# Five of the first seventeen edge groups get keys and values from gathered node rows instead of gathered table rows

## The chip, the cores and the metric

The kernel runs on one NeuronCore of a Trainium2 chip. The metric is device time in microseconds (us) of one execution. The engines are named as in the profile: PE (matrix products), DVE (vector), ACT (scalar), POOL and SP (here issuers of DMAs, POOL of the indirect ones). The time before is the median of ten runs.

## The reference, cut to what matters

A graph of 3125 nodes with 128 features has 100000 edges, sorted by destination; each edge has one of five relations. There are eight heads of 16 features.

```
for r in range(5):
    q = x[dst] @ W_Q[r];  k = x[src] @ W_K[r];  v = x[src] @ W_V[r]     # per edge
    logits = (q * k).sum(-1) / 4 + attn_bias[r]                         # per edge and head
    attn = softmax of logits over the edges of type r with the same dst
    out += segment_sum(attn * v, dst)                                    # per node
h = out @ out_proj_w.T + out_proj_b + x
x = layernorm(x + layernorm(h) * gamma + beta)
```

## The kernel before, in words

**Build.** For each of 25 blocks of 128 nodes, `turn` transposes the block (L301, L303) and `table` (L312) multiplies it by keys' and values' weights of all five relations; the rows of 256 numbers go to a table in HBM, `kv_d`, one row for each node and relation (store at L319, issued by SP). Between the blocks, the list `side` puts preparation: `rows_of` (L327 to L337) finds for each node which stretch of 500 destinations (SR) holds its first edge, `in_row` (L341) reads that stretch by an indirect DMA of POOL, `count` (L349, ACT) counts in it; the others make the indices `idx`, the places `nkey` and the types, and check the input. The small parameters are loaded after the build (L489 to L494).

**First queries.** For blocks 0 to 2 the nodes are loaded again, turned, multiplied by the query weights (L546, L556), split into three bf16 parts (L561 to L575), and stored to `q_d` (L579), one block after the other.

**Groups.** The edges are handled in 196 groups of 512 (g, 4 tiles of 128 edges). `gather(g)` (L527 to L533) issues four indirect DMAs on POOL, each bringing 128 rows of `kv_d` into one of KVB = 24 buffers. `fetch` (L584 to L590) loads keys and a window of 128 query rows; `spot` (L594) makes one-hot matrices; `spread_q` (L603, twelve bf16 products) brings queries to edges; `logits` (L616, L617) multiplies and reduces; `store_logits` (L622) writes them to `lg_d`. For each block b of nodes, `maxima_load` (L629), an indirect DMA on POOL too, loads the logits of each node's edges as the tile `ell`, and `maxima` (L636 to L673), in two halves, takes the maxima by relation. The weighing of group v then takes `spread_m` (L693), `less_max`, `exps`, `weigh` (L710), `places` (one-hot matrices on ACT, L728 and L731, or on DVE, L723) and `sums` (L744), with the running sum of the group before carried in by a fifth product (L748) from a fifth one-hot plane of `at`. `norm`, `by_node`, `project`, `residual`, `roots` and `norms` finish the nodes.

**Order.** All is unrolled and ordered by hand in steps k; each engine and each DMA queue works in the order in which the loop from L911 issues. Group g has its logits in step `step_of[g]`, which is g, plus one extra step after each group in CATCH_UP = (186, 188, 190, 192, 194). Gathers are issued AHEAD = 3 steps before use, one step before use in the last 16. The load of block b stands on POOL's queue in step `full_step[b] + 1`: the first behind the gathers of group 12, the second behind those of group 21. They need the logits up to group 8 and group 17. The first weighing is in step 16, and steps run to 223; the last group has its logits in step 200 and its weighing in step 214. The gather of group g + 24 must wait until group g has been weighed.

Of the kernel before, what the change touches and what calls it, by code (L numbers as in the profile page):

```python
# [8 lines left out]
F32 = mybir.dt.float32  # L9
# [38 lines left out]
CATCH_UP = (186, 188, 190, 192, 194)  # L48
# [7 lines left out]
SR = 500  # L56
NSR = E // SR
KVB = 24
# [58 lines left out]
def windowed_path(  # L117
# [13 lines left out]
    key_d = dram.tile([NGR, GE], BF16, name="key_d")  # L131

# [5 lines left out]
    nkey = keep("nkey", [P, T + 1, NGR])  # L138
# [11 lines left out]
    wq = keep("wq", [P, R, H])  # L150

# [15 lines left out]
    nc.vector.memset(xn[:, NT - 1, :], 0.0)  # L167
    fr = load.tile([1, NGR + NSR], I32, name="fr")
# [16 lines left out]
    nc.sync.dma_start(xn[:, :4, :], x[: 4 * P].rearrange("(i p) h -> p i h", p=P))  # L185
# [7 lines left out]
    def load_rows(name, a, pad):  # L193
        t = load.tile([HG, 2, GE], I32, name=name)
        nc.vector.memset(t[:, 1, :], pad)
        nc.scalar.dma_start(t[:, 0, :], a[: HG * GE].rearrange("(g i) -> g i", i=GE))
        nc.scalar.dma_start(
            t[: HR - 1, 1, :], a[HG * GE : (NGR - 1) * GE].rearrange("(g i) -> g i", i=GE)
        )
        rest = E - (NGR - 1) * GE  # L200
        nc.gpsimd.dma_start(
            t[HR - 1 : HR, 1, :rest], a[(NGR - 1) * GE :].rearrange("(g i) -> g i", g=1)
        )
        return t
# [30 lines left out]
    mid = iota("mid", [[P * E // N, NT]], NT)  # L235
    five = iota("five", [[R, WN]], WN, mult=-1)
# [21 lines left out]


    wkv = load.tile([P, R, 2, H], F32, name="wkv")  # L260
# [14 lines left out]
    firsts = load.tile([P, NGR + NSR], F32, name="firsts")  # L275
    frf = load.tile([1, NGR + NSR], F32, name="frf")

    def begins():
        nc.vector.tensor_copy(frf, fr)
        fp = pps.tile([P, NGR + NSR], F32, name="fp", tag="tr", bufs=2)  # L280
        nc.tensor.matmul(fp, ones[0:1, :], frf, start=True, stop=True)
        nc.vector.tensor_copy(firsts, fp)
        nc.vector.tensor_copy(first, frf[:, :NGR])
        nc.vector.tensor_scalar_mul(first5, frf[:, :NGR], float(R))
        nc.vector.tensor_tensor(
            nkey[:, T, 1:], firsts[:, 1:NGR], firsts[:, : NGR - 1], op=ALU.subtract
        )
        nc.vector.tensor_scalar(
            nkey[:, T, 1:], nkey[:, T, 1:], float(R), row_of, op0=ALU.mult, op1=ALU.subtract
        )  # L290
# [7 lines left out]

    def turn(b):
        tp = pps.tile([P, P], F32, name="tp", tag="tr", bufs=2)  # L300
        nc.tensor.transpose(tp, xn[:, b, :], ident)  # L301
        xT = work.tile([P, P], F32, name="xT", bufs=4)
        nc.vector.tensor_copy(xT, tp)  # L303
        return xT
# [21 lines left out]
    def rows_of(c0, c1):  # L326
        less = work.tile([P, 5, NSR], BF16, name="less", bufs=1)  # L327
        nc.vector.tensor_tensor(
            less,
            firsts[:, None, NGR:].to_broadcast([P, 5, NSR]),  # L330
            node[:, c0:c1, None].to_broadcast([P, 5, NSR]),
            op=ALU.is_lt,
        )
        g = grp[:, c0:c1]
        nc.vector.tensor_reduce(g, less, AX.X, ALU.add)
        nc.vector.tensor_scalar(g, g, 1.0, 0.0, op0=ALU.subtract, op1=ALU.max)
        nc.vector.tensor_copy(grp_i[:, c0:c1], g)  # L337
# [57 lines left out]
    def put_key(ep, g):  # L395
        nc.scalar.mul(nkey[:, :T, g], ep, -1.0)
# [38 lines left out]
    def checks():  # L435
# [16 lines left out]

    side = {
        0: [begins],
        1: [lambda: rows_of(0, 5)],
        2: [lambda: rows_of(5, 10), lambda: rows_of(10, 15)],
        3: [lambda: rows_of(15, 20)],
        4: [lambda: rows_of(20, NT)],
        5: [keys_a],
        6: [keys_c],  # L460
        7: [lambda: along(kvrow, 0, put_idx)],
        8: [lambda: along(kvrow, 1, put_idx)],
        9: [keys_b],
        11: [lambda: along(keyr, 0, put_key)],
        12: [lambda: along(keyr, 1, put_key)],
        13: [lambda: along(typr, 0, put_typ)],
        14: [lambda: along(typr, 1, put_typ)],
        16: [sorted_rows],
        18: [sorted_ends],
        21: [starts],  # L470
        23: [checks],
    }
    rows, counted = {}, 0
    xT = {b: turn(b) for b in range(2)}
    for b in range(NT):
        if b + 2 < NT:
            xT[b + 2] = turn(b + 2)
        table(b, xT.pop(b))
        for f in side.get(b, ()):
            f()  # L480
        while len(rows) < min(NT, 5 * b) and len(rows) - counted < 8:
            rows[len(rows)] = in_row(len(rows))
        for n in range(2):
            if b >= 3 and counted < len(rows):
                count(counted, rows[counted])
                counted += 1


    nc.scalar.dma_start(beta_t, beta.partition_broadcast(P))  # L489
    nc.scalar.dma_start(gamma_t, gamma.partition_broadcast(P))  # L490
    ow = load.tile([P, H], F32, name="ow")
    nc.scalar.dma_start(ow, out_w)
    nc.scalar.dma_start(bias4, attn_bias.partition_broadcast(P))
    nc.scalar.dma_start(lift, out_b.rearrange("(o h) -> o h", o=1))  # L494
    nc.vector.tensor_scalar_mul(bias4, bias4, 4.0)
    nc.vector.tensor_tensor(lift, lift, beta_t[0:1, :], op=ALU.subtract)
    op_ = pps.tile([P, P], F32, name="op_", tag="tr", bufs=2)
    nc.tensor.transpose(op_, ow, ident)
    nc.scalar.copy(out_wT, op_)
# [27 lines left out]
    def gather(g):  # L527
        kv = kvs_[g % KVB]
        for t in range(T):
            nc.gpsimd.indirect_dma_start(  # L530
                out=kv[:, t, :], out_offset=None, in_=kv_d[:, :],
                in_offset=bass.IndirectOffsetOnAxis(ap=idx[:, t, g : g + 1], axis=0),
            )  # L533


    def fetch_x(name, b):
        n = min(P, N - b * P)
        xb = flow.tile([P, H], F32, name=name, bufs=2 if name == "xq" else 4)
        if n < P:
            nc.vector.memset(xb, 0.0)  # L540
        nc.sync.dma_start(xb[:n], x[b * P : b * P + n, :])
        live[name, b] = xb
# [41 lines left out]
    def fetch(g):  # L584
        kt = flow.tile([P, T, P], BF16, name="kt", bufs=3)
        nc.sync.dma_start(kt.rearrange("w t p -> w (t p)"), key_d[g].partition_broadcast(P))
        qw = flow.tile([P, 3, H], BF16, name="qw", bufs=3)
        f = window(g, first5, SPE)
        nc.sync.dma_start(qw.rearrange("w s h -> w (s h)"), q_d[bass.ds(f, P), :])
        live["kt", g], live["qw", g] = kt, qw  # L590
# [22 lines left out]
    def logits(g):  # L613
        kv, lg = kvs_[g % KVB], live["lg", g]
        prod = flow.tile([P, T, H], F32, name="prod")
# [11 lines left out]
    def maxima_load(b):  # L627
        ell = late_flow.tile([P, D, LW], F32, name="ell")
# [7 lines left out]
    def maxima(b, c0, c1):  # L636
# [17 lines left out]
        wl = late_flow.tile([P, RH, HEADS, D], F32, name="wl", bufs=1)  # L654
# [33 lines left out]
    def spread_m(g):  # L688
        me = ps.tile([P, T, HEADS], F32, name="me")
# [27 lines left out]
    def places(g, on_dve):  # L717

        at = late_flow.tile([P, T + 1, WR], F32, name="at", bufs=3)
        n = T if g == 0 else T + 1  # L720
        for t in range(n):
# [9 lines left out]
        nc.scalar.activation(  # L731
            at[:, on_dve:n, :], at[:, on_dve:n, :], AF.Relu, bias=1.0, scale=-1.0
        )
        live["at", g] = at

    def sums(g, done):
# [3 lines left out]
        if g is not None:  # L740
            at, wv = live.pop(("at", g)), live.pop(("wv", g))
            pp = both[:WR, :PW]
            for t in range(T):
                nc.tensor.matmul(  # L744
                    pp, at[:, t, :], wv[:, t, :], start=(t == 0), stop=(t == T - 1 and g == 0)
                )
            if g:
                nc.tensor.matmul(  # L748
                    pp, at[:WR, T, :], live.pop(("pt", g - 1)), start=False, stop=True
                )  # L750
            live["pp", g] = pp
# [46 lines left out]
    def residual(b):  # L798
# [6 lines left out]
        h = late_flow.tile([P, H], F32, name="h", bufs=4)  # L805
# [49 lines left out]
    def lag(b):  # L855

        return LAG if b < NT - 3 else LAG - 2
# [21 lines left out]

    q_from = []  # L880
# [9 lines left out]
    first_b = [b for b in range(NT) if q_from[b] < 2]  # L890
    for b in first_b:
        fetch_x("xq", b)
        turn_q(b)
        turned(b)
        for c0, c1 in ((0, RH), (RH, R)):
            queries(b, c0, c1)
            first_part()
            remainder()
            second_part()
            third_part()  # L900
        store_q(b)
    nc.scalar.dma_start(
        m_d.rearrange("(p a) c -> p (a c)", p=P), oT.bitcast(BF16)[:, : NT * R * 3 * HEADS]
    )
    for g in range(3):
        fetch(g)
# [4 lines left out]
    for k in range(root_at[NT] + 2):  # L911
        v, g = v_at.get(k), group_at.get(k)
        q_step = {k - f: b for b, f in enumerate(q_from) if b not in first_b and -2 <= k - f <= 5}

        if k + 3 in group_at:
            fetch(group_at[k + 3])
# [11 lines left out]
        for u in range(NGR):  # L928
            if max(at_k[u] - 3, ready[block_of(u)] - 2) == k:
                fetch_m(u)  # L930

# [6 lines left out]

        for b in range(NT):
# [34 lines left out]
        if v_at.get(k + 1) is not None:  # L974
            places(v_at[k + 1], 3 if k >= final - 1 else 0)
# [11 lines left out]
        for b in range(NT + 1):  # L987
            if root_at[b] == k:
                roots(b)
                norms(b)  # L990
        if 0 in q_step:
# [510 lines left out]
```

## Time and profile before

| what | us |
|---|---|
| median of 10 runs (1213.93 to 1219.82) | 1215.58 |
| the profiled execution, its own time | 1217.49 |
| its span in the trace | 1215.7 |
| last table store issued by SP (L319) | 96.5 |
| first gather on POOL (L530) | 101.30 |
| first logits (L616), group 0 | 142.43 |
| logits of group 17 (L616) | 195.67 |
| second load of `ell` on POOL (L629) | 213.42 |
| last gather on POOL | 1131.51 |
| last weighing (L710), group 195 | 1194.91 |

The span falls into the build (0 to 101 us), the groups ahead of the first weighing (to about 190 us), the long middle in which each block of eight groups takes 41.5 us, and the end, which is free of gathers. POOL is busy for 806.0 us, DVE for 937.2, ACT for 728.9, and PE for 806.3. Busy shares are means over these stages.

### The profile page before, as it was taken

To read this page: it belongs to the slowest core of one execution; us is meant where nothing else is said; L and a number is where in the kernel's file an instruction comes from. 1 tells how busy PE (TensorE), PEld (TensorE's weight loads), DVE (VectorE), ACT (ScalarE), POOL (GpSimd) and SP (SyncE) were. 2 spreads that over 40 slices of the span, in tenths; PEclk is the share of its full clock that TensorE was granted. 3 is DMA by queue.
4 is the path that set the end of the run, shared out by engine and by line. 5 is a ranking of instruction groups with operands and counts; after the bars stand their busy time and mean duration, and the time that the engine had idled before them with its cause. 6 is when DMAs were issued, how large, how long until landed. Compare 5 with 4: busy or idle time off the path is not lost.

```text
span 1215.7 us, 25279 instructions
## 1 busy us (share of the span) xinstructions
PE 806.3 (66%) x7503; PEld 698.3 (57%) x7503; DVE 937.2 (77%) x2521; ACT 728.9 (60%) x2441; POOL 806.0 (66%) x902
## 2 busy tenths in 40 slices
PE   5793356558566766767576767566765777668674
PEld 2351236457466655666576657566665667657664
DVE  4742376777888888879888888888888888877775
ACT  1561015357666766766677667666766776669443
POOL 2715777777777777777777777777777777774200
PEclk9896566777678787877887687878877877768666
DMA  7984777667667766776676677677676767655200
GB/s 168 325 328 147 212 215 184 148 181 191 158 171 183 181 170 171 184 178 168 175 191 167 170 180 192 156 172 184 173 178 163 191 172 174 172 138 127 51 9 14
DMA packets 181075, 207.02 MB, mean 170 GB/s; under 512 B 82614, under 2 KB 145871, under 8 KB 180808
## 3 DMA queue, kind: packets, MB, share of 16 engines
q0 software_dynamic: 41392, 116.59, 35.4%
q1 hardware_dynamic: 135112, 84.01, 27.8%
q10 hardware_dynamic: 4424, 4.71, 1.6%
q8 instruction: 62, 1.02, 0.3%
q14 instruction: 85, 0.70, 0.2%
HBM read 169.90 MB, written 35.29 MB: 169 GB/s over the span
## 4 chain that ended last, share of the span: by engine, by line
DVE 28%; DMA 26%; POOL 14%; issue 12%; PE 11%; ACT 8%; SPq 1%; ACTq 0%; DVEq 0%; POOLq 0%
POOL kv L530 13%; DMA kv<-kv_d,idx 11%; DMA ell<-lg_d,start_i 7%; DVE wl L656 4%; DVE lg L617 4%; DVE prod L616 3%; PE pp L744 3%; DVE wv L710 3%; ACT at L728 3%; PE pr L312 2%; DVE mx L662 2%; DVE hot L594 2%; DMA kt<-key_d 1%; PE qe L603 1%; DVE o L769 1%
## 5 line engine op out<-in xcount | busy, mean ns | idle before, releaser
L530 POOL DMA_INDIRECT kv<-kv_d,idx x784 | 747.2, 953 | 274.4 <-issue 194.3
L744 PE MATMUL pp<-wv,at 128*125 128x136 f32 x1568 | 304.2, 351 | 16.5 <-DVE o L769 14.8
L728 ACT ACTIVATE at<-row_at,nkey 128x125 f32<-128x125 f32 x934 | 292.0, 390 | 0.0
L744 PEld LDWEIGHTS pp<-wv,at 128*125 128x125 f32 x1568 | 257.8, 239 | 24.8 <-DVE o L769 17.1
L603 PE MATMUL qe<-qw,hot 125*128 125x128 bf16 x2352 | 211.8, 255 | 30.7 <-DMA qw<-q_d 17.1
L603 PEld LDWEIGHTS <-hot 125*128 125x128 bf16 x2352 | 198.7, 125 | 35.7 <-issue 12.2
L693 PE MATMUL me<-mw,hot 125*128 125x8 bf16 x2352 | 91.3, 168 | 185.1 <-DVE wv L710 124.3
L693 PEld LDWEIGHTS <-hot 125*128 125x128 bf16 x2352 | 83.2, 101 | 223.5 <-DVE wv L710 134.9
L704 ACT ACTIVATE me<-me 128x32 f32<-128x32 f32 x196 | 36.2, 185 | 218.2 <-DVE me L700 217.4
L616 DVE TENSOR_TENSOR prod<-kv,qe 128x512 f32<-128x512 f32 x196 | 134.4, 686 | 36.0 <-PE qe L603 21.8
L710 DVE TENSOR_TENSOR wv<-kv,me 128x512 f32<-128x512 f32 x196 | 133.2, 680 | 20.1 <-ACT wv L705 20.0
L731 ACT ACTIVATE at<-at 128x625 f32<-128x625 f32 (+2 forms) x196 | 137.5, 702 | 6.2
L617 DVE TENSOR_REDUCE lg<-prod 128x32 f32<-128x512 f32 x196 | 134.5, 686 | 6.8
L748 PE MATMUL pp<-pt,at 125*125 125x136 f32 x390 | 101.7, 351 | 29.8 <-ACT pt L760 27.6
L556 PE MATMUL prq<-wq,xTq 128*128 128x384 f32 (+1 forms) x100 | 57.0, 665 | 85.3 <-DVE rem L566 84.1
L748 PEld LDWEIGHTS pp<-pt,at 125*125 125x125 f32 x390 | 79.4, 247 | 35.4 <-ACT pt L760 32.7
L594 DVE TENSOR_SCALAR hot<-kt,row_of 125x512 bf16<-125x512 bf16 x196 | 72.3, 369 | 16.3 <-DMA kt<-key_d 16.3
L754 PEld LDWEIGHTS pp<-rsum,o 125*128 125x128 f32 x392 | 80.1, 248 | 2.2 <-ACT oT L779 1.4
L656 DVE TENSOR_TENSOR wl<-by_head,shut 128x1536 f32<-128x1536 f32 (+1 forms) x50 | 74.6, 1491 | 7.6 <-ACT by_head L641 5.8
L556 PEld LDWEIGHTS prq<-wq,xTq 128*128 128x128 f32 x100 | 21.7, 271 | 94.9 <-DVE rem L566 92.8
L662 DVE TENSOR_REDUCE mx<-wl 128x24 f32<-128x1536 f32 (+1 forms) x50 | 74.3, 1487 | 1.7
L754 PE MATMUL pp<-rsum,o 125*128 125x25 f32 x392 | 71.8, 266 | 2.0 <-DVE o L769 1.3
(158 smaller groups left out, 1006.3 us busy)
## 6 DMA issues: line engine op xcount, KB each, us to landing
kt<-key_d SPq DMA_DIRECT2D x196, 128.0 KB
qw<-q_d SPq DMA_DIRECT2D x196, 96.0 KB
kv_d<-kvs SPq DMA_DIRECT2D x24, 640.0 KB
kv<-kv_d,idx POOLq DMA_INDIRECT x784
q_d<-q SPq DMA_DIRECT2D x25, 480.0 KB
lg_d<-lg SPq DMA_DIRECT2D x196, 18.0 KB
mw<-m_d SPq DMA_DIRECT2D x196, 6.0 KB
xq<-in_x SPq DMA_DIRECT2D x24, 64.0 KB
```

The source lines that it names most:

```text
L530: nc.gpsimd.indirect_dma_start(out=kv[:, t, :], out_offset=None, in_=kv_d[:, :], in_offset=bass.IndirectOffsetOnAxis(ap=idx[:, t, g : g + ...
L603: nc.tensor.matmul(qe[:, t, :], hot[:, t, :], qw[:WR, s, :], start=(s == 0), stop=(s == 2))
L616: nc.vector.tensor_tensor(prod, kv[:, :, :H], live.pop(("qe", g)), op=ALU.mult)
L617: nc.vector.tensor_reduce(lg[:, :, :HEADS], prod.rearrange("p t (k d) -> p t k d", d=HD), AX.X, ALU.add)
L656: nc.vector.tensor_tensor(wl[:, :n], by_head[:, None].to_broadcast([P, n, HEADS, D]), shut[:, :n, None, :].to_broadcast([P, n, HEADS, D]), ...
L693: nc.tensor.matmul(me[:, t, :], hot[:, t, :], mw[:WR, s, :], start=(s == 0), stop=(s == 2))
L710: nc.vector.tensor_tensor(wv[:, :, :H].rearrange("p t (k d) -> p t k d", d=HD), kv[:, :, H:].rearrange("p t (k d) -> p t k d", d=HD), live ...
L728: nc.scalar.activation(at[:, t, :], row_at[:, :WR], AF.Abs, bias=nkey[:, t, g : g + 1], scale=1.0)
L731: nc.scalar.activation(at[:, on_dve:n, :], at[:, on_dve:n, :], AF.Relu, bias=1.0, scale=-1.0)
L744: nc.tensor.matmul(pp, at[:, t, :], wv[:, t, :], start=(t == 0), stop=(t == T - 1 and g == 0))
L748: nc.tensor.matmul(pp, at[:WR, T, :], live.pop(("pt", g - 1)), start=False, stop=True)
L754: nc.tensor.matmul(op, live.pop(("o5", done)), rsum[:WR], start=True, stop=True)
```

## The change: what it does

**Early groups.** XG is the groups 4, 7, 10, 13 and 16. `gather` does nothing for them. Ahead of the row reads of the build, POOL issues 20 indirect DMAs that gather the source nodes' rows of x themselves (512 bytes a row) by `xi`, a list loaded straight from `src`. After the last table store, SP stores them to `x_d` (five stores of 256 KB). For group u, two steps before step u - 4 (for group 4 ahead of the steps), SP loads `xe` from there, and the edge types `tr` as a row given to all partitions. In step u - 4, `turn_x` transposes four tiles on PE, and `by_relation` makes five masked copies on DVE, `xm`. In step u - 3, `products` issues 20 f32 products of 256 columns, which add up over the five relations. In step u - 2, `put_kv` copies keys and values into the buffer of the group on ACT. The tile `xm` has the buffer of the tile `wl` of `maxima` (one buffer, tag "wl"); `tx` and `pk` have the two PSUM buffers of `me`.

**First queries.** The turned blocks 0 to 2 of the build are kept, multiplied by the query weights at once after the last table, in six products that follow each other, and stored.

**Carry.** The fifth plane of `at` goes; a table `carried`, made once in the build, holds for each group a plane of five columns, and the product of the carry is issued ahead of the last of the four products of `sums`.

**Build.** SR is 250; `rows_of` looks at three stretches around the expected one for all blocks at once; the small loads move into the build; the first blocks of x come ahead of the other loads, and a small copy on ACT ahead of the weights.

**Steps.** CATCH_UP is empty, so the last group has its logits in step 195; the last three blocks have a lag of seven steps instead of six. The last weighing is still in step 214, and steps still run to 223. Four blocks instead of three have their roots put off until after the last weighing. `places` puts two planes on DVE instead of three in the end. `xr` and `h` have three buffers, `prod` and `ell` one.

```diff
-CATCH_UP = (186, 188, 190, 192, 194)
+CATCH_UP = ()
-SR = 500
+SR = 250
+SB = P * E // N // SR
+SPAD = 5
+XG = range(4, 17, 3)
+QB = 3
...
+    def rows_of():
+        less = load.tile([P, NT, 3, SB], F32, name="less")
+        rows = firsts.rearrange("p (b s) -> p b s", s=SB)
+        for i in range(3):
+            nc.vector.tensor_tensor(
+                less[:, :, i, :], rows[:, i : i + NT, :],
+                node[:, :, None].to_broadcast([P, NT, SB]), op=ALU.is_lt,
+            )
+        nc.vector.tensor_reduce(grp, less.rearrange("p b i s -> p b (i s)"), AX.X, ALU.add)
...
+    def early_x():
+        i, t = pieces.pop(0)
...
+        nc.gpsimd.indirect_dma_start(
+            out=staged[i][:, t, :], out_offset=None, in_=x[:, :],
+            in_offset=bass.IndirectOffsetOnAxis(ap=xi[:, i, t : t + 1], axis=0),
+        )
...
+    for n in range(20):
+        early_x()
     rows, counted = {}, 0
...
+    put_x(NT)
...
+    for i in pieces:
+        b, c0, c1 = i
+        pr = pps.tile([P, 4, H], F32, name="pr", tag="pr", bufs=4)
+        prs[i] = pr[:, : c1 - c0, :]
+        nc.tensor.matmul(prs[i], kept[b], wq[:, c0:c1, :], start=True, stop=True)
+        nc.scalar.copy(q3s[b][:, c0:c1, 0, :], prs[i])
...
     def gather(g):
+        if g in XG:
+            return
...
+    def by_relation(g):
+        tr, tx = live.pop(("tr", g)), live.pop(("tx", g))
+        xm = late_flow.tile([P, R, T, P], F32, name="xm", tag="wl", bufs=1)
+        for r in range(R):
+            nc.vector.scalar_tensor_tensor(
+                xm[:, r], tr.rearrange("h (p t) -> h t p", t=T), float(r), tx,
+                op0=ALU.is_equal, op1=ALU.mult,
+            )
+    def products(g, t0):
+        xm = live["xm", g]
+        pk = ps.tile([P, 2, KVW], F32, name="pk", tag="me")
+        for t in range(2):
+            for r in range(R):
+                nc.tensor.matmul(
+                    pk[:, t, :], xm[:, r, t0 + t, :], wkv[:, r].rearrange("h s c -> h (s c)"),
+                    start=(r == 0), stop=(r == R - 1),
+                )
+    def put_kv(g, t0):
+        nc.scalar.copy(kvs_[g % KVB][:, t0 : t0 + 2, :], live.pop(("pk", g, t0)))
...
-        n = T if g == 0 else T + 1
-        for t in range(n):
+        for t in range(T):
...
+                if t == T - 2 and g:
+                    nc.tensor.matmul(
+                        pp[:R], carried[:WR, g, :], live.pop(("pt", g - 1)),
+                        start=False, stop=False,
+                    )
...
-        return LAG if b < NT - 3 else LAG - 2
+        return LAG if b < NT - 3 else LAG - 1
...
+    x_at = {g: step_of[g] - 4 for g in XG}
...
-            places(v_at[k + 1], 3 if k >= final - 1 else 0)
+            places(v_at[k + 1], 2 if k >= final - 1 else 0)
```

## Prediction

> **What bounds the kernel now.** First the busy shares by engine: DVE 77%, POOL 66%, nothing near full, so the share alone names no limit. Second the waits of POOL over the whole span:
>
> ```profile
> POOL kv L530 <- issue: 194.3, 637, 0.3
> ...
> POOL ell L629 <- DMA mw<-m_d: 16.7, 1, 16.7
> POOL ell L629 <- ACT lg L610: 13.5, 1, 13.5
> POOL kv L530 <- DMA kv<-kv_d,idx: 9.1, 30, 0.3
> ```
>
> The columns are us in total, times, longest. 637 of the 784 gathers "wait" 0.3 us for nothing that the profile shows: that is the pace of POOL itself. Third its timeline, around the second load of `ell`:
>
> ```profile
> 212.17 0.94 POOL L530 DMA_INDIRECT kv<-kv_d,idx  x1 [0.30 <-issue]
> 213.42 0.95 POOL L629 DMA_INDIRECT ell<-lg_d,start_i  x1 [0.30 <-issue]
> 214.67 0.95 POOL L530 DMA_INDIRECT kv<-kv_d,idx  x1 [0.31 <-issue]
> ```
>
> One indirect DMA takes 0.95 us and the next follows 0.30 later. From the first gather (101.30) to this load stand 89 of them, 112.1 us, so 1.26 us each. The two long waits of the first view stand at 1121 and 1149, in the end. From 101 to 1107 POOL is a chain without a hole (one of 1.9 us): **POOL's count of indirect DMAs is the bound**. Fourth the windows, to see who has room:
>
> ```profile
> 120.00:150.00 30.00, 8.83 (x60) 6.22 (x61) 8.77 (x17) 2.82 (x12) 22.79 (x24) 0.56 0.71 207
> ...
> 180.00:200.00 20.00, 12.57 (x116) 10.65 (x116) 12.90 (x31) 11.09 (x38) 15.12 (x17) 0.50 0.66 176
> ...
> 600.00:800.00 200.00, 138.63 (x1448) 127.07 (x1448) 169.73 (x463) 140.31 (x472) 151.55 (x159) 0.77 0.71 176
> ```
>
> Behind each stretch: its length, busy us of PE, PE's weight loads, DVE, ACT, POOL, then PE's granted clock, DMA share, GB/s. In the middle DVE is at 85%. Fifth DVE's waits between 400 and 1000:
>
> ```profile
> DVE sd L817 <- ACT sd L812: 22.5, 15, 1.6
> DVE mine L643 <- DMA ell<-lg_d,start_i: 20.0, 12, 2.9
> ```
>
> DVE waits about 1.7 us a block for an `ell` that POOL issued in its turn, and never there for a gather to land. So the weighing side is only some 4% (1.7 of 41.5) faster than POOL: a second limit close behind.
>
> **The sum** is made on the span, 1215.7 us; this execution's own time is 1217.49, the median 1215.58, so that a saving on the span is taken off the median unchanged.
>
> *A. Build: -6 (0 to -9).* The old `rows_of` costs DVE five times 1.19 + 1.20 (L328, L335) and small ones, 13 us, while tables wait. The new one is three comparisons of 400 and a sum over 1200 elements: by 0.69 for 512 (L616) and 1.22 for 1024 (L369) about 3, and `carried` 1.2. But POOL, free at 8.1 and used at 30.2 before, first issues 20 gathers of x: 8.2 + 20 x 1.26 = 33.4. That covers them all but 3 us; then come 25 row reads to 65, the last landing near 67.5. Two are counted per table, which holds table 15 there. Nine tables at the cadence of L312 (74.81 to 77.07: 2.26) end at 88; I add 2.5 for stores in the way (one took 7.3 at 62.9): 90.5 for the last store, against 96.5. Bounds: no gain if table stores bind (640 KB per table; 340 GB/s between 60 and 90), -9 without that 2.5 and another 0.5.
>
> *B. Twenty gathers less: -25.2*, 20 x 1.26, all ahead of the second `ell`. Without further waits this load would go at 213.4 - 25.2 - 6 = 182.2.
>
> *C. New waits of POOL at `ell`: +13 (0 to +56).* That load needs the logits of group 17. First queries: before, three blocks in series, the last stored at 131.14, first logits 11.3 later, at 142.4. Now nothing is fetched; from the last table ACT has 3 x (0.48 + 0.37 + 0.51 + 0.40) = 5.3, with first product and DVE some 8, then 11.3 again, and 2 for 1.3 MB of `x_d` stores: first logits at 90.5 + 8 + 11.3 + 2 = 111.8.
> Then each early group is a chain over three steps: `spread_q` 0.84 (L603 x12), logits 1.45, `spot` 0.35, first mask 0.7, then the other masks beside the first tile's products 3.2, then 15 products. The masks are priced at 0.69 (L616, f32 from PSUM; L379 with int32 inputs gives half of 1.22). A product of 256 columns of f32: L312 does 1280 columns in 2.15, so 0.43; 15 make 6.5. Together 13.0. With three chains, 2 for block 3's queries and 1.8 for the first logits, the fourth masking (group 13) begins at 111.8 + 1.8 + 39 + 2 = 154.6. Now `maxima` of block 0 falls in: its `wl` shares a buffer with `xm` and waits for the products (10.4), then 1.76 + 1.75, logits and `spot` 1.8, second half 4.3 (0.6, 1.23, 1.22, six of 0.2): 20, to 174.6. Group 16's masks and products 10.4, `spread_q` 0.84, three logits with what lies between 7: logits of 17 end at 192.8; from logits to `ell` the end of this trace shows 2.4 (1146.8 to 1149.2). The load goes at 195.2 instead of 182.2. It waits 13, partly already at the first load (after logits 8); 18.2 of the saving are left. Behind it POOL is the chain of before, from group 22 on. The lower end is no wait. The upper one is PE at half its pace throughout: 0.43 more on each of 100 products, 43 on top.
>
> *The clock row.* After a gap the six instructions of L312 take 4.17 us, six us later 2.31:
>
> ```profile
> 18.74 4.17 PE L312 MATMUL pr<-wkv,xT 128*128 128x512 f32 x6 [2.49 <-ACT wkv L272]
> ...
> 24.56 2.31 PE L312 MATMUL pr<-wkv,xT 128*128 128x512 f32 x6
> ```
>
> In my chain PE stands still some 1 us between masks, so I take the warm value. [...]
>
> *D. The end: -1 (-7 to +9).* Before, 28 steps from the logits of 186 (1082.2) to the last weighing (1194.9) hold both long waits of POOL. After: nine steps with groups at POOL's pace, 9 x 5.04 + two `ell` 2.5 = 47.9, from 1077.6 (the maxima of block 22, 4.6 here, come a step later); then 19 steps of 2.79 (weighings 185 to 195: 1166.99 to 1194.91), 53, and maxima 13.2: 1191.7, 3.2 less. One more root behind the last weighing costs 2.5 (1201.72 to 1204.2); `xr` with three buffers must wait for one of these roots, about 1; the smaller `places` gives back a little. Bounds: 7 less if these steps keep 2.55 as the fastest do, 9 more if the 3 us load of `xr` (1203.71 in the chain) and two more waits for `ell` stand bare.
>
> *At nothing:* the fifth plane saves ACT 0.39 + about 0.15 in each of 196 steps, where ACT is at 70% in the middle and off the bound; if POOL did not cover it, it would be worth the 0.6 that DVE waits at L710 per block. The carry product comes 0.29 earlier in its accumulation and may wait for the copy `pt` by as much (L748 waits 22.6 in 800 us); DVE covers it. `put_kv`, two ACT copies of 0.59, ends a step before use.
>
> Sum: -6 - 25.2 + 13 - 1 = -19.2: **1196 us**.
>
> **Rivals.**
> *1. POOL never waits at `ell`.* For it: PE's bare work per three steps is 8.6 + 2.5 + 0.7 = 11.8, gathers take 10.1, and queries may start sooner than 111.8. Against: one buffer for `xm` and `wl`. C falls away: 1183.
> *2. The weighing side binds.* The chain takes 15.5 instead of 13 (cold starts, strided masks), 12.5 more over five, or, being only 4% faster than POOL, it does not catch up the 9 us that it is later against POOL than in the middle (where `ell` goes 12 us after the logits it needs). 1208.
> *3. Slower: PE at low clock in the 100 products.* Place: between logits 0 and 17. The granted clock stands at 0.56 and 0.50 around that stretch before (windows above, with PE mostly idle). Price: 43 at half clock, 1239; it decides once the mean product takes more than 0.43 + 19.2/100 = 0.62 us. Against: PE now has work nearly without a break there, and had clock 1.00 when that was so (60 to 90 us).
> *4. The change does not act:* excluded; the new order of instructions has 764 gathers of `kv_d` and the 20 of x ahead of the row reads.
>
> **Chances and range.** Forecast (1188 to 1206) 0.47, rival 1 (1179 to 1187) 0.20, rival 2 (1207 to 1213) 0.18, near 1215 0.05, rival 3 0.10. Below 1180 and above 1214 I leave out no more than 2 in 10: 1180 to 1214. A run of this kernel can tell 0.2%, 2.4 us, from no change: faster 0.85, same 0.05, slower 0.10.
>
> **What would show it.** A: SP's last table store near 90. B: 764 gathers, first one near 95. C: a wait at the first two loads of `ell` of 13 us together, the second issued near 195, and products of 0.43 us at a clock near 1. D: last gather near 1105, last weighing near 1174. The forecast is wrong if POOL waits again and again after 200 us (rival 2), or if products take over 0.62 (rival 3).

## The result and the profile after

The changed kernel is slower: a median of 1229.76 us (1224.11 to 1232.93, 13 runs) against 1215.96 us (1211.55 to 1219.82, 46 runs) before, a ratio of 1.0106 (95% interval 1.0095 to 1.0118). The forecast was 1196, faster. The profiled span is 1228.2 us, 12.5 more than before. In four of the six sets of runs below the kernel before itself took 1624 to 1642 us instead of 1217 (once on a chip that gave 1217 in another set), so the runs of these "slow sets" are compared only inside one set.

POOL's waits after, in total, times and longest (us), show the two new ones at `ell` that the prediction priced at 13 together, and one in the end, where the kernel before waited 16.7 and 13.5:

```profile
POOL kv L629 <- issue: 188.6, 619, 0.3
POOL kv L629 <- DVE q3s L589: 34.9, 1, 34.9
POOL ell L776 <- DVE lg L764: 18.2, 1, 18.2
POOL ell L776 <- DMA kt<-key_d: 12.9, 1, 12.9
POOL ell L776 <- DVE shut L798: 7.0, 1, 7.0
```

The two new ones are 12.9 and 18.2, 31.1 in sum (7.0 is the one in the end). POOL's timeline gives the place of the longer one, the second load, which was issued at 213.42 before and not held up:

```profile
220.29 0.94 POOL L776 DMA_INDIRECT ell<-lg_d,start_i  x1 [18.22 <-DVE lg L764]
```

**The balance of the span**, from the starts of the same instructions in both traces:

| at | before | after | difference |
|---|---|---|---|
| first gather | 101.30 | 103.33 | +2.0 |
| second load of `ell` | 213.42 | 220.29 | +6.9 |
| load of `ell` of block 21 | 1043.80 | 1049.75 | +6.0 |
| last weighing | 1194.91 | 1204.05 | +9.1 |
| end of the span | 1215.7 | 1228.2 | +12.5 |

At the second load 2.0 - 25.2 (20 gathers of 1.26) + 31.1 (waits) = 7.9, and 6.9 stands there. The middle gives back 0.9: POOL's pace is that of before. The end, in which a gain of 1 was forecast, costs 6.6. A window of the changed kernel there (length, busy us of PE, weight loads, DVE, ACT, POOL, then PE's granted clock, DMA share, GB/s):

```profile
1160.00:1190.00 30.00, 30.00 (x214) 23.90 (x214) 15.43 (x64) 13.37 (x59) 0.00 (x0) 0.50 0.03 5
```

From 1160 PE has no idle time in the records and a clock of 0.50; the same 30 us of the kernel before show:

```profile
1160.00:1190.00 30.00, 25.11 (x224) 24.49 (x223) 22.38 (x87) 15.69 (x67) 0.00 (x0) 0.62 0.05 9
```

So there are three questions: why the end has a slow PE, why the early groups make POOL wait 31 us, and why the build gained nothing.

### The profile page after: what moved, and what is told of

Same layout as the page of the kernel before. It is cut to its first block, busy times and chain, and to the rows that moved or that the text cites. A ratio compares the mean times of both kernels' runs of the same rounds, so it can differ in the third digit from the quotient of the medians.

```text
span 1228.2 us, 25732 instructions
## 1 busy us (share of the span) xinstructions
PE 905.5 (74%) x7722; PEld 705.6 (57%) x7722; DVE 951.2 (77%) x2531; ACT 653.8 (53%) x2257; POOL 799.8 (65%) x904
## 3 DMA queue, kind: packets, MB, share of 16 engines
q8 instruction: 64, 1.05, 0.3%
## 4 chain that ended last, share of the span: by engine, by line
DVE 30%; PE 24%; DMA 18%; POOL 11%; issue 10%; ACT 5%; SPq 1%; ACTq 0%; DVEq 0%; POOLq 0%
DMA kv<-kv_d,idx 12%; POOL kv L629 10%; PE pp L888 8%; DVE prod L763 4%; DVE lg L764 4%; PE pr L347 4%; DVE wv L857 4%; PE qe L750 3%; DVE wl L803 2%; PE pk L717 2%; DVE hot L741 2%; PE pp L890 2%; DVE mx L809 2%; DMA mw<-m_d 2%; ACT at L874 2%
## 5 line engine op out<-in xcount | busy, mean ns | idle before, releaser
L629 POOL DMA_INDIRECT kv<-kv_d,idx x764 | 724.8, 949 | 267.4 <-issue 188.6
L888 PE MATMUL pp<-wv,at 128*125 128x136 f32 x1568 | 375.9, 376 | 17.6 <-DVE o L912 12.7
L888 PEld LDWEIGHTS pp<-wv,at 128*125 128x125 f32 x1568 | 280.3, 246 | 86.3 <-issue 65.4
L874 ACT ACTIVATE at<-row_at,nkey 128x125 f32<-128x125 f32 x744 | 236.7, 391 | 0.0
L750 PE MATMUL qe<-qw,hot 125*128 125x128 bf16 x2352 | 202.3, 248 | 27.1 <-DMA qw<-q_d 19.7
L750 PEld LDWEIGHTS <-hot 125*128 125x128 bf16 x2352 | 191.0, 121 | 29.8 <-issue 20.2
L840 PEld LDWEIGHTS <-hot 125*128 125x128 bf16 x2352 | 85.9, 102 | 164.6 <-DVE wv L857 89.3
L763 DVE TENSOR_TENSOR prod<-kv,qe 128x512 f32<-128x512 f32 x196 | 133.9, 683 | 52.2 <-PE qe L750 47.1
L877 ACT ACTIVATE at<-at 128x500 f32<-128x500 f32 (+1 forms) x196 | 117.3, 599 | 6.2
L890 PE MATMUL pp<-pt,carried 125*5 125x136 f32 x390 | 95.9, 337 | 14.0 <-ACT pt L903 13.9
L655 PE MATMUL prq<-wq,xTq 128*128 128x384 f32 (+1 forms) x88 | 44.7, 600 | 75.7 <-DVE rem L665 75.7
L922 ACT COPY oT<-pp 128x25 f32 x196 | 33.4, 171 | 96.6 <-PE pp L897 51.0
```

Of the source, the lines that this page charges most:

```text
L629: nc.gpsimd.indirect_dma_start(out=kv[:, t, :], out_offset=None, in_=kv_d[:, :], in_offset=bass.IndirectOffsetOnAxis(ap=idx[:, t, g : g + ...
L750: nc.tensor.matmul(qe[:, t, :], hot[:, t, :], qw[:WR, s, :], start=(s == 0), stop=(s == 2))
L763: nc.vector.tensor_tensor(prod, kv[:, :, :H], live.pop(("qe", g)), op=ALU.mult)
L840: nc.tensor.matmul(me[:, t, :], hot[:, t, :], mw[:WR, s, :], start=(s == 0), stop=(s == 2))
L874: nc.scalar.activation(at[:, t, :], row_at[:, :WR], AF.Abs, bias=nkey[:, t, g : g + 1], scale=1.0)
L877: nc.scalar.activation(at[:, on_dve:], at[:, on_dve:], AF.Relu, bias=1.0, scale=-1.0)
```

## Experiments

Theory: the saving of 25 us is given back by the chain of masks and products of the early groups, and the end is late by its new order of steps. Rivals: the end is late by the new carry product; the chain would be caught up by a weighing side that limits anyway; the weights, on which PE starts at 16.6 instead of 10.1, make the build late.

### The end: order of steps or carry

**e1_tail** puts the old order back.

```diff
-CATCH_UP = ()
+CATCH_UP = (186, 188, 190, 192, 194)
-        return LAG if b < NT - 3 else LAG - 1
+        return LAG if b < NT - 3 else LAG - 2
```

> The changed kernel with the step order of before in the end: CATCH_UP = (186, 188, 190, 192, 194) and a lag of six steps for the last three blocks. Theory (the order of the steps costs the 6 us of the end): the steps that only weigh go from 19 back to 14, last gather about 1132 again, and the time falls by 5 to 7 us to about 1223.5. Rival (the new carry product with five columns keeps PE at a granted clock of 0.50, whatever the order): steps that only weigh keep 3.4 us each, the clock there stays at 0.50, and the time is 1228 to 1231.

Measured: 1235.73 us, ratio to before 1.0134 (1.0105 to 1.0164). The order is not the cost; the old one is worse. From the load of block 21 to the last weighing it takes 160.1 us (1051.46 to 1211.54) against 154.3 in the changed kernel, and the steps that only weigh keep 3.40 us. My theory of the end fell.

**e2_carry** puts the old carry back, with the fifth plane that ACT makes for it, and changes nothing else.

```diff
-                if t == T - 2 and g:
-                    nc.tensor.matmul(
-                        pp[:R], carried[:WR, g, :], live.pop(("pt", g - 1)),
-                        start=False, stop=False,
-                    )
+            if g:
+                nc.tensor.matmul(
+                    pp, at[:WR, T, :], live.pop(("pt", g - 1)), start=False, stop=True
+                )
```

> The changed kernel with the carry of before: a fifth plane of the one-hot tile made on ACT and a last product of 125 columns, no table of carries. Theory (order of the steps): the last 19 steps stay at 3.3 to 3.4 us, the time is within 2 us of 1229.8 (0.5 us of ACT more in each step lies beside other work). Rival (the carry product): granted clock between 1160 and 1190 rises from 0.50 to 0.6, steps fall to about 2.8 us, the time falls by 8 to 11 us to about 1220.

Measured: 1219.11 us, ratio to before 1.0013 (0.9999 to 1.0027): 10.7 us less than the changed kernel. PE's timeline in a step that only weighs, first the changed kernel (start, duration; each f32 product is two records):

```profile
1169.61 0.62 PE L890 MATMUL pp<-pt,carried 125*5 125x136 f32 x2
1170.15 0.82 PE L888 MATMUL pp<-wv,at 128*125 128x136 f32 x2
1170.77 0.46 PE L897 MATMUL pp<-rsum,o 125*128 125x25 f32 x2
1171.05 0.47 PE L840 MATMUL me<-mw,hot 125*128 125x8 bf16 x12
```

and then the kernel with the old carry:

```profile
1168.50 0.44 PE L836 MATMUL me<-mw,hot 125*128 125x8 bf16 x12
1169.21 1.19 PE L887 MATMUL pp<-wv,at 128*125 128x136 f32 x8 [0.27 <-DVE o L912]
1170.24 0.40 PE L891 MATMUL pp<-pt,at 125*125 125x136 f32 x2
1170.48 0.30 PE L897 MATMUL pp<-rsum,o 125*128 125x25 f32 x2
```

The carry takes 0.62 with five columns and 0.40 with 125, and all the other products are longer beside it: by the starts of the weighings most of these steps take 3.40 or 3.41 us there and 2.35 to 3.02 here. The five columns themselves are not dear: at 220.40 us of the changed kernel the same carry takes 0.40 too. Its window from 1160 has the clock at 0.78, although PE has less recorded work in it:

```profile
1160.00:1190.00 30.00, 27.14 (x274) 25.89 (x274) 21.38 (x87) 23.58 (x92) 0.00 (x0) 0.78 0.04 5
```

With the old carry, the end from the load of block 21 (1050.36) takes 167.8 us to the span's end, 171.9 before, 178.5 in the changed kernel. So the rest of the new end (order of steps, roots, buffers) saves 4.1 and the new carry costs 10.6. The same end takes 165.2 in e10b below, so the 4.1 is uncertain by some 3 us; the 10.6 agrees with the medians, which are 10.7 apart.

**e5_mid**, repeated as **e5b_mid**, **e5c_mid** and **e5d_mid**, parts the two things that the new carry has: it keeps the old plane of 125 columns and takes only the new place.

```diff
-                        pp[:R], carried[:WR, g, :], live.pop(("pt", g - 1)),
+                        pp, at[:WR, T, :], live.pop(("pt", g - 1)),
                         start=False, stop=False,
```

> The changed kernel with the carry's plane of 125 columns as before, but issued where the change has its carry: ahead of the last of the four products of a group instead of behind it. Theory 1 (the place in the accumulation costs: PE waits for pt with a product still to come, so the last product lies on the chain from one group's sum to the next): as slow as the changed kernel, 1228 to 1231, granted clock 0.50 between 1160 and 1190. Theory 2 (the stationary of five columns keeps the granted clock low): as fast as the kernel with the carry of before, 1218 to 1221, clock near 0.78 there.

> The carry's plane of 125 columns issued ahead of the last product, once more, on a chip where the kernel before takes its usual time. Theory 1 (the place in the accumulation): 1228 to 1231, granted clock 0.50 between 1160 and 1190. Theory 2 (the stationary of five columns): 1218 to 1221, clock near 0.78 there.

> The carry's plane of 125 columns issued ahead of the last product. Theory 1 (the place in the accumulation): as slow as the changed kernel, 1228 to 1231, granted clock 0.50 between 1160 and 1190. Theory 2 (the stationary of five columns): 1218 to 1221, clock near 0.78 there.

> The carry's plane of 125 columns issued ahead of the last product, on a chip where the kernel before takes its usual time. Theory 1 (the place in the accumulation): as slow as the changed kernel, 1228 to 1231, granted clock 0.50 between 1160 and 1190. Theory 2 (the stationary of five columns): 1218 to 1221, clock near 0.78 there.

All four fell in slow sets: 1675.2, 1658.9, 1656.0 and 1655.7 us, ratios to before 1.0188, 1.0171, 1.0194 and 1.0203 (all intervals within 1.0128 to 1.0258). The times can't be held against the expectations, but the clock in the end can be held against that of e7 and e8 below, which ran in three of the same sets and have the five columns in the same place. A stretch of 25 us among the steps that only weigh, ending some 25 us ahead of the span's end, in e5d_mid:

```profile
1600.00:1625.00 25.00, 22.41 (x223) 21.25 (x222) 17.48 (x71) 19.28 (x76) 0.00 (x0) 0.77 0.03 3
```

and of e7c_one_mask, in the same set:

```profile
1624.00:1649.00 25.00, 25.00 (x172) 19.61 (x172) 13.19 (x54) 11.48 (x49) 0.00 (x0) 0.50 0.01 1
```

The four runs with 125 columns have 0.77 to 1.00 there, the six with five columns 0.50 each, with PE recorded as busy throughout and 172 or 173 product records instead of 223 to 258. So it is the columns (the width of the stationary, the operand of the weight-load records: 125x5 at L890 of the changed kernel), not the place. One thing is not parted from them: with the 125 columns ACT makes its fifth plane again (ACT is busy for 19.28 instead of 11.48 us above). Five columns in the last place were not tried.

And the five columns alone are not enough. In the middle the same carry runs in every step, and the clock is 0.76, against 0.77 in the kernel before and 0.78 in e2:

```profile
600.00:800.00 200.00, 151.59 (x1400) 121.20 (x1399) 167.34 (x453) 121.79 (x423) 151.06 (x160) 0.76 0.69 174
```

From 704 to 712 it stands at 1.00. Of the stretches of 20 us from 100 us on, only the three from 1140 to 1200, where PE has the weighing alone, have 0.50 in the changed kernel; the others have 0.59 to 1.00. Why the five columns go with the low clock there stays open.

### The early groups

**e4_one_rel** leaves out masks and products of four of the five relations (so its early groups are not complete).

```diff
-        for r in range(R):
+        for r in range(1):
```

(in `by_relation` and in `products`)

> The changed kernel with the mask and the product of one relation only in the early groups; the masks and products of the other four relations are left out (4 masks of 0.97 us and 16 products of 0.43 us less for each of five groups). Theory (the waits at the first two loads of ell come from this chain, and POOL is the only bound behind them): the waits of 12.9 and 18.2 us shrink to under 5 together, the second load of ell goes at 192 to 196, and 25 to 28 us of it reach the end: 1203. Rival (the weighing side cannot run that far ahead): the second load is as early, but POOL waits again later, and the time is 1212 to 1220.

Measured: 1203.43 us, ratio to before 0.9872 (0.9848 to 0.9897). Of the waits at the first two loads of `ell` 4.0 us are left, at the second:

```profile
152.58 0.95 POOL L776 DMA_INDIRECT ell<-lg_d,start_i  x1 [0.30 <-DVE hot L741]
193.02 0.94 POOL L776 DMA_INDIRECT ell<-lg_d,start_i  x1 [3.99 <-DMA xq<-in_x]
```

The second load goes at 193.02, 27.3 sooner than in the changed kernel, and 26.3 of it reach the end. So the weighing side would have followed, and it is the chain of the first groups that holds POOL.

**e7_one_mask** (with **e7b_one_mask**, **e7c_one_mask**) leaves out four masks and keeps 20 products; **e8_one_prod** (with **e8b_one_prod**, **e8c_one_prod**) leaves out 16 products and keeps five masks.

```diff
-        for r in range(R):
+        for r in range(1):
...
-                    pk[:, t, :], xm[:, r, t0 + t, :],
+                    pk[:, t, :], xm[:, 0, t0 + t, :],
```

```diff
-            for r in range(R):
+            for r in range(R - 1, R):
```

(the second in `products`, where each product then starts and ends its own sum)

> The changed kernel with one mask instead of five for each early group; the 20 products stay and all read that mask (the masks of four relations are left out). If DVE's masks bind the chain of the first groups (they take 4.9 us a group and hold up everything behind them on DVE): the second load of ell goes at 201 to 205 instead of 220.3, that is 15 to 19 us sooner. If PE's products bind it: at 213 or later.

> One mask and 20 products for each early group (the masks of four relations are left out), once more. If DVE's masks bind the first groups: second load of ell at 201 to 205 instead of 220.3. If PE's products bind them: at 213 or later.

> One mask and 20 products for each early group (the masks of four relations are left out). If DVE's masks bind the first groups: second load of ell at 201 to 205 instead of 220.3. If PE's products bind them: at 213 or later; the chips on which everything was slow point to this (5 to 6 us sooner there).

> The changed kernel with four products instead of twenty for each early group, with all five masks (the products of four relations are left out). If PE's products bind the chain of the first groups (20 products of 0.43 us and cold starts): the second load of ell goes at 200 to 206 instead of 220.3. If DVE's masks bind it: at 213 or later. If masks and products stand one behind the other, this kernel and the one with a single mask together gain about the 27 us that the kernel with one relation gained there (193.0).

> Five masks and four products for each early group (the products of four relations are left out), once more. If PE's products bind the first groups: second load of ell at 200 to 206 instead of 220.3. If DVE's masks bind them: at 213 or later. If the two stand one behind the other, their gains add up to the 27 us of the kernel with one relation.

> Five masks and four products for each early group (the products of four relations are left out). If PE's products bind the first groups: second load of ell at 200 to 206 instead of 220.3; the chips on which everything was slow point to this (18 us sooner there). If DVE's masks bind them: at 213 or later. If the two stand one behind the other, their gains add up to the 27 us of the kernel with one relation.

All in slow sets: 1692.6, 1679.5 and 1676.0 us with one mask, 1681.9, 1667.4 and 1666.4 with one product. From the first gather to the second load of `ell` e5, with all masks and products, takes 178.1, 177.8 and 178.1 us in these sets; one mask takes 4.3, 5.3 and 8.3 less, one product 21.4, 22.9 and 23.1 less. So there both count, and the products more. But how much of it holds at the usual pace is not shown: in the three e5 runs PE stands idle for 16.7 to 18.7 us ahead of products of the chain with nothing to wait for in the profile ("issue"), in the changed kernel for none in this stretch, and leaving out products leaves out most of these holes (in front of the products that are left, 4.4 us in e8b and none in e8 and e8c). That the gains add up to 26 to 31, near the 26.1 that e4 gains over the same stretch at the usual pace (117.0 to 90.9), can be chance.

**e9_kv** (with **e9b_kv**) has the old carry, and `xm` in the buffers of the groups 21 to 23, so that it shares nothing with `wl`.

```diff
-        xm = late_flow.tile([P, R, T, P], F32, name="xm", tag="wl", bufs=1)
+        xm = [
+            kvs_[KVB - 3 + r // 2][:, :, r % 2 * H : r % 2 * H + H] for r in range(R)
+        ]
```

> The changed kernel with the carry of before and with the masked copies xm in the buffers of the groups 21 to 23, which no gather needs yet, so that they share nothing with wl. Theory (sharing costs the 5.5 us that wl waits for the products, and the masks of group 16 that wait for wl): the second load of ell goes 4 to 7 us sooner than in the kernel with the carry of before (218.4), at 211 to 214, and the time is 1212 to 1215. Rival (the chain of masks and products is as long without the sharing): the load within 1.5 us of 218.4, time 1218 to 1220.

> Carry of before and xm in the buffers of the groups 21 to 23, once more. Theory (sharing a buffer with wl costs 4 to 7 us): second load of ell at 211 to 214 instead of 218.4 with the carry of before alone, time 1212 to 1215. Rival (masks and products are as long without the sharing): the load within 1.5 us of 218.4, time 1218 to 1220.

Both in slow sets: 1663.8 and 1649.7 us, ratios 1.0142 (1.0092 to 1.0192) and 1.0117 (1.0093 to 1.0141). From first gather to second load they take 170.7 and 172.0, 7.4 and 5.8 less than e5 in the same sets, where the carry doesn't yet act. That looks like the theory, but the sharing is not what `wl` waits for. In e9 and e9b it still waits 15.9 and 20.8 us (27.8 and 25.1 in e5 and e5b), for `by_head`, a copy that ACT makes; and the gathers of the new buffers now wait for the products (19.3 and 4.3 us in e9b). The changed kernel has the same wait, 5.52 at 184.23 us (shown below), and ACT's timeline gives its reason:

```profile
182.53 0.58 ACT L726 COPY kv<-pk 128x512 f32<-128x512 f32 x1 [3.73 <-PE pk L717]
...
183.10 1.09 ACT L788 COPY by_head<-ell 128x512 f32<-128x512 f32 x1
```

On ACT `put_kv` stands ahead of `by_head`, and it waits for the last product of the early group. So no run shows that the sharing costs anything; a kernel with `by_head` ahead of `put_kv` was not run.

**e10_kv_g3** and **e10b_kv_g3** are e9 with three early groups.

```diff
-XG = range(4, 17, 3)
+XG = range(4, 11, 3)
```

> Carry of before, xm in the buffers of the groups 21 to 23, and three early groups (4, 7, 10) instead of five. Theory (the first groups are a serial chain of 14.5 us for each early group and the two groups behind it, against 10.1 us of gathers for those two, so that five early groups make POOL wait and three hardly do): 12 gathers are saved, 15.1 us; the second load of ell goes at 199 to 204 and the time is 1202 to 1207, below the kernel before. Rival (each early group less costs its 5 us, and the wait stays): second load at 212 to 220, time 1216 to 1222.

> Carry of before, xm in the buffers of the groups 21 to 23, three early groups (4, 7, 10). Theory (five early groups are a chain longer than the gathers beside it, three hardly are): 12 gathers are saved, 15.1 us; the second load of ell goes at 199 to 204 and the time is 1202 to 1207, below the kernel before. Rival (the wait stays as long with three): second load at 212 to 220, time 1216 to 1222.

The first, in a slow set: 1640.7 us, ratio 1.0099 (1.0078 to 1.0121). The second, at the usual pace: 1206.1 us, ratio to before **0.9904** (0.9880 to 0.9927), below both kernels, at the time expected but not for the reason expected. POOL's timeline at the first and the second load:

```profile
163.24 0.94 POOL L774 DMA_INDIRECT ell<-lg_d,start_i  x1 [9.91 <-DMA lg_d<-lg]
...
210.21 0.95 POOL L774 DMA_INDIRECT ell<-lg_d,start_i  x1 [0.30 <-ACT at L873]
```

The second load no longer waits, but it goes at 210.2, not 199 to 204: the first still waits 9.9 us, because the masks of group 10 stand before the logits of group 8 that it needs. Of 15.1 us of gathers saved, and with the first gather 2.1 later, only 3.2 are left there (213.42 to 210.21). The other 6.7 of the 9.8 us on the span come from the end: 165.2 us from the load of block 21, 171.9 before. The old kernel with the new order of steps alone was not run.

### The build

**e3_wfirst** issues the query weights as SP's first load (L178), the rest unchanged.

```diff
+    wn = load.tile([3 * R * HEADS, H * HD], F32, name="wn")
+    for s, a in enumerate((w_k, w_v, w_q)):
+        (nc.sync if s == 2 else nc.scalar).dma_start(
...
     nc.sync.dma_start(xn[:, :4, :], x[: 4 * P].rearrange("(i p) h -> p i h", p=P))
```

> The changed kernel with the query weights as the first load on SP, ahead of x, xi and the begins. Theory (the weights' landing at 16.3 instead of 10.1 sets the whole build, where PE's products follow each other): PE starts near 10 us, the last table store goes near 93 instead of 99, first gather near 97.5, both loads of ell 5 to 6 us sooner, time 1224. Rival (the begins of 250 stretches, now landing later, or the table stores bind the build): first gather within 1.5 us of 103.3, time 1228 to 1230.

Measured: 1230.55 us, ratio 1.0102 (1.0084 to 1.0121), no change from the changed kernel. PE starts at 9.51 instead of 16.59 and the first table at 18.65 instead of 22.50, but the lead is gone by the thirteenth table. PE's timeline there, e3 first:

```profile
62.76 0.70 PE L347 MATMUL pr<-wkv,xT 128*128 128x256 f32 x2 [0.78 <-ACT kvs L351]
...
63.85 2.31 PE L347 MATMUL pr<-wkv,xT 128*128 128x512 f32 x6
```

The changed kernel starts the same table at the same time:

```profile
63.84 2.38 PE L347 MATMUL pr<-wkv,xT 128*128 128x512 f32 x6
```

On the way PE waits in e3 for ACT's copies of the tables (2.06 at 43.17, 1.10 at 59.01, 0.78 at 62.76), while ACT counts (L386, 0.49 + 0.19 each) and issues the key stores and the small loads that now stand in the build (55.97 to 61.06). The first gather is at 103.27. ACT's counts wait in turn for the row reads of POOL (1.92 at 39.90, 1.56 at 42.05, 1.15 at 47.72). So the weights' landing doesn't set the end of the build; that row reads and ACT do in the middle is read from the trace, not tested.

## Why the prediction was wrong, point by point

Forecast was -19.2 on the span, found +12.5: 31.7 apart. A is 8.0 of it, C 18.1 and D 7.6; the middle gives back 0.9, and the sum at the second load is 1.0 too high.

**What bounds the kernel: right.** A shift of POOL at the second load reached the end in e4 (27.3 to 26.3), and the middle kept its pace in every run at the usual pace.

**A, the build: wrong in sign.** -6 forecast, +2.0 found at the first gather (the last table store was issued at 98.6, not 90.5). The failing step is the one that held tables only by the row reads and then let nine follow at 2.26; the tables are late before that. The table that starts at 37.30 is the fourth here and was the sixth before; at 64 us the changed kernel is still one behind (the 13th at 63.84, the 14th at 64.32 before). PE is busy for 38.26 of the 40 us from 40 to 80 (36.69 before), so there is little room to catch up. What a faster build would have needed was not tested.

**B, 20 gathers: right.** 764 gathers, 25.2 us.

**C, the waits at `ell`: the term that was mis-sized,** 31.1 instead of 13. From first gather to second load 99.9 us were forecast (195.2 - 95.3) and 117.0 found, 17.1 more. The first logits came 19.2 after the first gather instead of 16.5 (2.7). The rest is the chain, 97.8 instead of 83.4. DVE's timeline after:

```profile
153.60 4.96 DVE L706 SCALAR_TENSOR_TENSOR xm<-tr,tx 128x512 f32<-128x512 int32 x5
...
169.92 4.93 DVE L706 SCALAR_TENSOR_TENSOR xm<-tr,tx 128x512 f32<-128x512 int32 x5
...
184.23 1.76 DVE L803 TENSOR_TENSOR wl<-by_head,shut 128x1536 f32<-128x1536 f32 x1 [5.52 <-ACT by_head L788]
...
193.44 4.93 DVE L706 SCALAR_TENSOR_TENSOR xm<-tr,tx 128x512 f32<-128x512 int32 x5
```

A mask takes about 0.97 by the starts (five in 4.94), not 0.69, so the first three periods are 14.46, 14.47 and 16.32 instead of 13, 13 and 15: 4.3. The period with the maxima is 23.5 instead of 20: 3.5. The prediction let `wl` start as soon as the products are done; it starts 1.7 later, behind `put_kv` and `by_head` on ACT (above), and `put_kv` was costed at nothing. From the fifth set of masks to the load it is 26.9 instead of 20.6: 6.3. The products hardly answer for it (start, duration; two records each):

```profile
158.61 7.17 PE L717 MATMUL pk<-wkv,xm 128*128 128x256 f32 x32 [0.27 <-DVE xm L706]
...
194.63 11.55 PE L717 MATMUL pk<-wkv,xm 128*128 128x256 f32 x40 [3.77 <-DVE xm L706]
```

In the third group four products keep step with the masks (from 154.73) and 16 follow in 7.17, 0.45 each: the price of 0.43 was right, and rival 3 had no ground. All 20 take 11.05 there and 11.55 in the last group, which starts at a clock of 0.50 (194.6 to 198.0). From the masks to the end of the last products it is 12.7 instead of 10.4. More is lost behind them: the logits of group 17 end at 214.5, but their store, which the load needs, is issued only at 217.67, since on SP a store of queries stands ahead of it:

```profile
216.35 0.34 SPq L678 DMA_DIRECT2D q_d<-q  x1
...
217.67 0.39 SPq L769 DMA_DIRECT2D lg_d<-lg  x1
```

From logits to load it is 5.8 instead of 2.4. (The releaser in the row of the load is the logits of group 19, which end as the load starts; it needs those up to 17.) With the first 0.3 these make the 14.4. Rival 2 had the mechanism, a chain longer than 13, but put it at 15.5, an estimate that no row of before shows, and the time at 1208; what it left out was A and D, and the queues of ACT and SP.

**D, the end: wrong in the item costed at nothing.** The order was forecast at -3.2 up to the last weighing with steps of 2.79; with the old carry it is -6.7 there (151.1 to 144.4), the lower bound of D, and +2.7 behind it (20.8 to 23.5) for roots and loads. The items of D as written (-3.2, +2.5, about +1) come to +0.3 and not -1 without a size for what `places` gives back. But the prediction put the five-column carry under "at nothing" because DVE would cover a wait of 0.29. The cost is not that wait: in the steps that only weigh all products on PE run at 0.50, steps take 3.40, and PE, not DVE, becomes the bound of the end, 10.6 us (e2).

Against rival 3 the prediction argued that PE had clock 1.00 when it worked nearly without a break (from 60 to 90 us of the kernel before, busy for 28.58 of 30). In the end of the changed kernel it was not so: PE is recorded as busy for 30.00 of 30 us from 1160 to 1190 and keeps 0.50.

The forecast of 1196 would have needed both: e4, with hardly any chain, still has the slow carry and takes 1203.

## What to carry to other kernels

Where work is taken from the bounding queue into a stage that other engines run in series, compare the new chain's period with the time of the queue's own work beside it (14.5 us against 10.1 here), for the stage's real distance to the wait that it feeds; three early groups lost 9.9 of 15.1 us, five lost more than they saved. Look at the order of the queues that the chain passes (ACT, SP), and not only at the prices of its parts. A product with fewer columns was not a cheaper one here (in the end 0.62 us with five, 0.40 with 125): look at the clock of the stage in which PE has no other work. And an item costed at nothing needs the stage in which its cover is gone, here the end without gathers.

## What the runs showed of the hardware

In the steps that only weigh, one product in five with a stationary of five f32 columns went with a granted clock of 0.50 on PE, through steps with no recorded idle time; with 125 columns the same steps ran at 0.77 to 1.00 in the four e5 runs and at 0.78 in e2. In the middle, among other products, the clock was 0.76 with the same five columns. Masks over 128x512 elements with an int32 operand started 0.97 us apart on DVE in a row of five and took 1.05 each as recorded, where the f32 product of the logits over as many elements (L763) took 0.68.
